# Decay layer of a four-layer graph kernel: counts of two groups share a bank, sums use the array's row halves, and the seams around it are rearranged

## The chip, the core and the metric

The kernel runs on one core of a Trainium2 chip. The metric is the time of one execution on the device in microseconds, as the median of several runs. The core has a matrix engine (PE; its weight loads are listed as PEld), a vector engine (DVE), a scalar engine (ACT), GpSimd (POOL) and a sync engine (SP) that here only issues DMAs. Each of them works through its own queue in order, and they wait for each other by semaphores. PE writes to PSUM, eight banks of 128 partitions x 512 fp32; DVE and ACT read PSUM. SBUF is the memory on the core.

## What is computed

Four layers run one after the other on node features x (4096 x 64) with one adjacency matrix adj (4096 x 4096), and each ends with a layer norm of x plus the layer's output:

```python
x = _layernorm(x + _L0_gnn_ref(x, adj, L0_gnn_weight), axis=-1)   # Chebyshev terms: x, L x, 2 L(..) - .., three products with adj
x = _layernorm(x + _L1_gnn_ref(x, adj, adj, ...), axis=-1)         # attention: products with (adj > 0), (adj < 0) and adj, two GRU cells
x = _layernorm(x + _L2_gnn_ref(x, adj, L2_gnn_weight, L2_gnn_bias), axis=-1)   # decay layer
x = _layernorm(x + _L3_gnn_ref(x, adj, L3_gnn_weight, L3_gnn_bias), axis=-1)   # hyperbolic layer
```

The decay layer, around which the change turns, is

```python
support = input @ weight
mask = (adj != 0)
rank = cumsum(mask, axis=1); deg = rank[:, -1:]
k = minimum(deg, 100.0); pos = rank - (deg - k)
w = mask * where(pos > 0, 0.5 ** (k - pos), 0.0)
out = w @ support + bias                # the kernel sums w @ input first and multiplies by weight after
```

So of each row of adj only the last 100 neighbours count, and each weighs half of the one after it.

## The kernel before

adj is cut into 8 groups of 512 rows, and each group into 8 chunks of 512 columns; a chunk has 4 blocks of 128 columns. Pass 1 (L526 to L575) loads adj chunk by chunk into the pool `rows0` (five buffers of 1 MB), transposes it on PE (L536), copies it out on ACT (L543), reduces it twice on DVE (L569, L571) and writes the transposed chunk to DRAM (L567) for the later layers. The product of the first Chebyshev term runs beside it. The first load is issued by SP at L169, once the constants are set up; the pool takes the SBUF space that the pool `tri` of the constants (L123) has left.

Passes 2 and 3 read the transposed chunks back (`load0`, L587). Pass 3 goes through the groups in the order 7, 0, 1, ..., 6; group g needs chunks g to 0. After a group's matmuls (`halves`, L436) comes `after_third`: the sums are copied out by ACT (`out_of`, L447), weighed and added to what the other terms gave (`times`, L467), normed on DVE (L608, `layernorm`, `centre` with L261, `split` into three bf16 parts L215 to L219), and one group later the result is transposed on PE (`turned_third`, L201). Each of these is put behind the next group's first tile by the small class `Behind`. Group 6, the last, is turned in attention.

Attention (L870 on, in one of two branches chosen by a value of the device) loads the chunks again, makes a mask of the positive entries on DVE (`positives`, L665), writes the mask to DRAM by a POOL DMA (`keep_mask`, L669) and runs three kinds of matmul on it (`wide` L906, 128*128 in the array; `narrow` L914, 128*64; `weighed` L923, 128*64 fp32). When a group's sums are complete, the small work of `group_end` follows in steps, one per chunk; its last step (`decay_parts`) splits the group's layer output into three bf16 parts, hi and mid beside each other in `sup_two`, lo in `sup_lo`.

The decay layer works on four groups at a time (two turns) and from the last column to the first, in 32 blocks of 128 columns a turn, each in two halves of 64 (`h`, odd and even). The count of the neighbours that follow is one matmul with a triangular constant `follow` on the mask, whose result (L1095) is at once the exponent of the weight; the count of group q stands in its own bank `cnt_ps{q}`, in 64 of its partitions (the lower or upper half of the array's columns), and the matmul of the next half block adds to it. The weight is read off the bits: a relu with scale -128 to a 16-bit integer, which is then taken for a bf16 (L1101 on ACT, L1103 on DVE, 64x512 each). So every half block has four count matmuls and four weight operations; ACT does groups 0 and 2 always, and group 3 in every second odd half. Both halves of a block fill one weight tile of 128 partitions, and six steps of two matmuls add the weights times hi, mid and lo to the sums (`gather`, L1064): two groups share a bank `acc_ps{a}`, one in each column half. The gathers of a block are issued among the counts of the next one, by a list `gathers`.

Beside this loop runs a list `seam`, one step a block (L1123): in the first turn the end of attention's last group (22 steps), in the second the ends of the first four groups of the decay layer: `copies` of the sums, `after_decay` for two groups at once (product with the weights L1039, bias, layer norm), `prepare` and `turn_prepared` for the next layer. The ends of the other four groups run in the hyperbolic layer.

The order on each engine is the order of the program as the framework's scheduler settles it; `in_order` pins the marked instructions to the order of the program.

Of the kernel before, what the change touches and what calls it, by code (L numbers as in the profile page):

```python
# [60 lines left out]
def gnn4_kernel(  # L61
# [36 lines left out]


# [60 lines left out]
    def gcols(g):  # L160
        return slice(g * GW, (g + 1) * GW)


    first_p = ctx.enter_context(ExitStack())
    rows_p = first_p.enter_context(tc.tile_pool(name="rows0", bufs=5))

    def load_raw(g, c):
        raw = rows_p.tile([P, GB, CB * P], F32, name="raw", tag="raw")
        nc.sync.dma_start(raw, adj[gcols(g), c * CB * P : (c + 1) * CB * P].rearrange("(b p) j -> p b j", p=P))  # L169
        return raw  # L170

    first_raw = [load_raw(0, NCH - 1)]
# [95 lines left out]
    wd = const.tile([P, 2 * F], F32, name="wd")  # L268
# [10 lines left out]
    def load_decay():  # L279
        nc.vector.memset(wd, 0.0)  # L280
        for q in range(2):
            nc.scalar.dma_start(wd[q * F : (q + 1) * F, q * F : (q + 1) * F], w_dec)
        nc.vector.tensor_scalar_mul(wd, wd, 2.0**DECAY_SHIFT)
        nc.scalar.dma_start(bd, b_dec.partition_broadcast(P))
# [115 lines left out]


# [5 lines left out]
    with first_p, tc.tile_pool(name="acc", bufs=1) as acc_p, tc.tile_pool(name="win", bufs=1) as win_p, tc.tile_pool(  # L407
# [64 lines left out]
        dpart = sm.tile([P, NG, NCH, GB], F32, name="dpart")  # L472
        lows = sm.tile([P, NG * NCH], F32, name="lows")
# [122 lines left out]
        def after_second(g, ps):  # L596
            gs = gblocks(g)
            t_v = out_of(ps, "t_v")
            o = times(new_post(), [(t_v, ident[:, 0:F])])
# [4 lines left out]
        def after_third(g, ps):  # L604
            gs = gblocks(g)
            o = times(new_post(), [(out_of(ps, "t_h"), cheb[:, 3, :]), (acc_t[:, g // 2, :], ident[:, mine(g)])])
# [26 lines left out]
        done = []  # L633
        for n, g in enumerate([NG - 1] + list(range(NG - 1))):
            ps = ps_a.tile([P, GW], F32, name="pass3", tag=("h_ps", "w_ps")[n % 2])
# [5 lines left out]
            while done:  # L641
                turned_third(done.pop())
            later.push(lambda g=g, ps=ps: [after_third(g, ps), done.append(g)])
        later.flush()
        not_turned = done.pop()

    three = ctx.enter_context(tc.tile_pool(name="three", bufs=1))

    nat_c = three.tile([P, NB, F], F32, name="nat_c")
# [6 lines left out]
    sup_two = late.tile([P, NB, 2 * F], BF16, name="sup_two")  # L656
    sup_lo = late.tile([P, NB, F], BF16, name="sup_lo")
    def load1(pool, g, c):
        at = pool.tile([P, CB, GW], F32, name="at1", tag="at")
        nc.sync.dma_start(at, adj_t[g][:, c * CB : (c + 1) * CB, :])  # L660
        return at

    def positives(pool, at):
        pos = pool.tile([P, CB, GW], MASK, name="pos")
        in_order(nc.vector.tensor_scalar(pos, at, 0.0, None, ALU.is_gt, saturate=False))  # L665
        return pos

# [19 lines left out]

# [5 lines left out]
    front = ctx.enter_context(ExitStack())  # L693
    front_p = front.enter_context(tc.tile_pool(name="front", bufs=1))
    with_at = [load1(front_p, NG - 1, c) for c in range(1)]
    with_pos = [positives(front_p, at) for at in with_at]


# [4 lines left out]
    def group_end(g, Q, nb, tl, sums, a_t, wq, by_ln=False):  # L703
# [142 lines left out]
        def decay_parts(ps_p):  # L846

            split(g, nat_b[:, gblocks(g), :], F, sup_two[:, :, 0:F], sup_two[:, :, F : 2 * F], sup_lo)
            nc.vector.tensor_tensor(
                nat_b[:, gblocks(g), :], nat_b[:, gblocks(g), :], bd.unsqueeze(1).to_broadcast([P, GB, F]), ALU.add  # L850
            )
# [18 lines left out]
    def attention(signed, cols_p, sg, tl, ps_a, ps_p):  # L870
# [3 lines left out]
        def masks(g, c):  # L874
            if g == NG - 1 and c < len(with_at):
                at, pos = with_at[c], with_pos[c]
            else:
                at, pos = load1(cols_p, g, c), None
# [17 lines left out]
            up = sg.tile([P, CB, GW], F32, name="up")  # L896
# [34 lines left out]
        else:  # L931
# [5 lines left out]
        lead = 1 if signed else 2  # L937
        ahead = [masks(*order[n]) for n in range(lead)]
        steps = [
            lambda ps_p: to_columns(  # L940
                ps_p, tr_a[0 : F + 1, gcols(not_turned)], nat_a[:, gblocks(not_turned), :], F + 1, nc.scalar.copy
            )
        ]
# [36 lines left out]
    for signed in (True, False):  # L980
        with tc.If(any_negative > 0) if signed else cmp.Else() as block:
            cmp = block
            with tc.tile_pool(name="cols1", bufs=4 if not signed else 2) as cols_p, tc.tile_pool(name="sign1", bufs=2 if signed else 5) as sg, tc.tile_pool(
# [4 lines left out]
                attention(signed, cols_p, sg, tl, ps_a, ps_p)  # L988

    front.close()  # L990
    nc.gpsimd.memset(tr_o, 0.0)
# [40 lines left out]

    decayed = {}

    def after_decay(ps_p, two):

        o = ps_p.tile([P, GB, 2 * F], F32, name="post", tag="post")
        for b in range(GB):
            nc.tensor.matmul(o[:, b, :], lhsT=decayed[two][:, cols(b)], rhs=wd, start=True, stop=True)  # L1039
# [12 lines left out]
    with tc.tile_pool(name="mask2", bufs=3) as mk_p, tc.tile_pool(name="wt2", bufs=3) as wt_p, tc.tile_pool(  # L1052
# [8 lines left out]
        def gather(part, jb, wt, acc, a):  # L1061
            parts = (sup_two[:, jb, 0:F], sup_two[:, jb, F : 2 * F], sup_lo[:, jb, :])
            for q in range(2):
                in_order(nc.tensor.matmul(  # L1064
                    acc[a][q * F : (q + 1) * F, :], lhsT=parts[part], rhs=wt[2 * a + q].bitcast(BF16),
                    start=(jb == NB - 1 and part == 0), stop=(jb == 0 and part == 2), skip_group_check=True,
# [8 lines left out]
        gathers = []  # L1075
        for turn, groups in enumerate(turns_of):
# [433 lines left out]
```

## Time and profile before

| | |
|---|---|
| three runs | 1586.68, 1585.27, 1582.21 us; median 1585.27 |
| the profiled execution | 1581.82 us, its span 1580.0 us, mean granted PE clock 0.968 |
| PE busy | 1418.8 us (90%), 6851 instructions |
| DVE busy | 1166.3 us (74%) |
| ACT busy | 820.1 us (52%) |
| POOL busy | 96.7 us (6%) |
| pass 1, about 12 to 361 us | DMA at 389 GB/s |
| passes 2 and 3, to 597 us | |
| attention, 604 to 887 us | |
| decay layer, 887 to 1108 us | |
| hyperbolic layer, to 1580 us | |

The profile is of one execution. A busy PE is not PE at its peak, since matmuls are pipelined: a matmul of 512 columns lasts some 380 ns in a row of the profile, while the next can start much earlier. The distance of two starts tells more. Rows of groups read: line, engine, operation, tiles out<-in, shape in the array (rows*columns, for PE), operands, count | busy us, mean ns of one | idle time of the engine before them and what ended it.

### The profile page before, as it was taken

Reading aid. Unit: us, or ns where it says so; the run is one execution under the profiler, and the core shown is the slowest. Engines: PE = TensorE matmul, PEld = TensorE weight load, DVE = VectorE, ACT = ScalarE, POOL = GpSimd, SP = SyncE. Lnnn points to the kernel's source line nnn. Section 1 sums busy time; section 2 is a strip of 40 time slices with the busy share of each in tenths; the row PEclk is TensorE's granted clock in tenths of the full one; section 3 lists DMA queues with packets and bytes.
Section 4 is the critical chain, followed back from the end, with each engine's and each line's share of the span. In section 5 each row is a group of like instructions: output and inputs, shape, how many; then the busy total and the mean of one; then the engine's idle time right before and its main releaser. Section 6 shows DMA issues by size and latency. Waiting matters only on the chain.

```text
span 1580.0 us, 19139 instructions
## 1 busy us (share of the span) xinstructions
PE 1418.8 (90%) x6851; PEld 691.3 (44%) x6874; DVE 1166.3 (74%) x2268; ACT 820.1 (52%) x1367; POOL 96.7 (6%) x162
## 2 busy tenths in 40 slices
PE   6899999999998987989999998789789999899995
PEld 4555555554443432333434444445333434344343
DVE  6788988982001534665676688888899999999997
ACT  3444444431000100222222588779888999898895
POOL 3001101000000001111111100000000000000000
PEclk9899999999999998999999999999899999999998
DMA  8999999996776778878978654442425444434430
GB/s 300 409 378 390 413 412 400 379 354 229 249 279 243 265 294 317 300 277 290 333 288 299 201 173 157 137 131 84 182 85 194 153 180 170 163 139 179 162 115 13
DMA packets 102336, 383.81 MB, mean 243 GB/s; under 512 B 15828, under 2 KB 16856, under 8 KB 70232
## 3 DMA queue, kind: packets, MB, share of 16 engines
q1 hardware_dynamic: 84256, 296.78, 52.9%
q0 software_dynamic: 14592, 84.16, 13.0%
q10 hardware_dynamic: 3384, 1.56, 0.5%
q8 instruction: 57, 0.93, 0.2%
q14 instruction: 47, 0.39, 0.1%
HBM read 297.26 MB, written 85.20 MB: 242 GB/s over the span
## 4 chain that ended last, share of the span: by engine, by line
PE 28%; DVE 22%; ACT 6%; DMA 2%; issue 2%; ACTq 0%; DVEq 0%; SPq 0%
PE v_ps L1227 6%; DVE wt L1103 5%; PE sums_ps L1287 4%; PE a_ps L923 3%; PE cnt_ps L1095 3%; DVE rt L1445 2%; DVE at_m L1273 2%; PE acc_ps L1064 2%; DMA at<-adj_t 2%; PE p_ps L906 2%; DVE f L1430 2%; PE post L729 1%; DVE at_d L1433 1%; DVE pos L665 1%; PE post L1271 1%
## 5 line engine op out<-in xcount | busy, mean ns | idle before, releaser
L543 ACT COPY at<-tp 128x512 f32<-128x512 f32 x256 | 133.0, 598 | 151.4 <-issue 106.2
L1101 ACT ACTIVATE wt<-cnt_ps 64x512 uint16<-64x512 f32 x288 | 163.1, 587 | 27.7 <-PE cnt_ps L1095 23.2
L1103 DVE TENSOR_SCALAR wt<-cnt_ps 64x512 uint16<-64x512 f32 x224 | 151.5, 692 | 29.6 <-PE cnt_ps L1095 23.8
L1227 PE MATMUL v_ps<-rv,tr_a 128*128 128x512 f32 (+1 forms) x288 | 142.2, 618 | 33.4 <-DVE rt L1445 32.5
L1095 PE MATMUL cnt_ps<-m,follow 128*64 128x512 fp8e4 x480 | 136.3, 390 | 23.1 <-DVE wt L1103 10.7
L569 DVE TENSOR_REDUCE dpart<-raw 128x4 f32<-128x2048 f32 x64 | 145.4, 2271 | 9.8 <-DMA raw<-in_adj_dram 9.8
L571 DVE TENSOR_REDUCE lows<-raw 128x1 f32<-128x2048 f32 x64 | 145.2, 2269 | 0.0
L536 PE MATMUL tp<-ident,raw 128*128 128x128 f32 x1024 | 133.7, 285 | 8.6 <-DMA raw<-in_adj_dram 8.6
L1287 PE MATMUL sums_ps<-at_d,nat_c 128*64 128x512 f32 x288 | 139.8, 606 | 1.4 <-DVE at_d L1433 1.0
L536 PEld LDWEIGHTS tp<-ident,raw 128*128 128x128 f32 x1024 | 117.2, 146 | 50.2 <-issue 41.2
L923 PE MATMUL a_ps<-at,nat_a 128*64 128x512 f32 x512 | 124.5, 613 | 2.9 <-DVE at L889 2.9
L665 DVE TENSOR_SCALAR pos<-at 128x2048 fp8e4<-128x2048 f32 x72 | 87.0, 1221 | 53.3 <-DMA at<-adj_t 43.4
L1292 PE MATMUL sums_ps<-at_m,nat_c 128*64 128x512 f32 x224 | 108.2, 605 | 0.0
L443 PE MATMUL w_ps<-at,cheb_n 128*128 128x512 f32 x224 | 101.1, 595 | 0.0
L443 PE MATMUL pass<-at,cheb_n 128*128 128x512 f32 x224 | 98.3, 596 | 0.7 <-DVE cheb_n L594 0.7
L1064 PE MATMUL acc_ps<-wt,sup_two 128*64 128x512 bf16 x512 | 96.6, 391 | 0.0
L1227 PEld LDWEIGHTS v_ps<-rv,tr_a 128*128 128x128 f32 x288 | 53.0, 199 | 83.9 <-DVE rt L1445 40.7
L1456 ACT ACTIVATE rt<-rt,one_col 128x1024 f32<-128x1024 f32 x72 | 78.7, 1094 | 17.4 <-DVE rt L1445 17.2
L1445 DVE SCALAR_TENSOR_TENSOR rt<-v_ps,rt 128x1024 f32<-128x1024 f32 x72 | 83.2, 1157 | 3.8 <-ACT rt L1421 3.6
L1430 DVE SCALAR_TENSOR_TENSOR f<-rt,w 128x1024 f32<-128x1024 f32 x72 | 82.8, 1158 | 3.3 <-ACT rt L1456 3.3
L1433 DVE TENSOR_TENSOR at_d<-at_d,f 128x1024 f32<-128x1024 f32 x72 | 83.2, 1156 | 0.1
L1273 DVE TENSOR_TENSOR at_m<-post,at_m 128x512 f32<-128x512 f32 x112 | 74.9, 683 | 9.6 <-PE post L1271 9.1
(346 smaller groups left out, 2262.3 us busy)
## 6 DMA issues: line engine op xcount, KB each, us to landing
at<-adj_t SPq DMA_DIRECT2D x122, 1024.0 KB, 5.2
raw<-in_adj_dram SPq DMA_DIRECT2D x64, 1024.0 KB, 12.1
adj_t<-at POOLq DMA_DIRECT2D x64, 1024.0 KB, 8.2
at_d<-adj_t SPq DMA_DIRECT2D x36, 1024.0 KB, 4.8
at_m<-adj_t SPq DMA_DIRECT2D x28, 1024.0 KB, 6.9
mask_t<-pos POOLq DMA_DIRECT2D x64, 256.0 KB, 6.1
m<-mask_t SPq DMA_DIRECT2D x120, 128.0 KB, 2.8
m<-mask_t SPq DMA_DIRECT2D x60, 256.0 KB, 4.1
```

What stands on the lines that cost most here:

```text
L443: in_order(nc.tensor.matmul(ps, lhsT=cheb_n[:, jb, k : k + 2, :], rhs=rhs, start=first, stop=last))
L536: in_order(nc.tensor.transpose(tp[:, cols(b)], raw[:, b, cols(k)], ident))
L543: nc.scalar.copy(at[:, k, :], tp)
L569: in_order(nc.vector.tensor_reduce(dpart[:, g, c, :], raw, AX.X, ALU.add))
L571: in_order(nc.vector.tensor_reduce(lows[:, n : n + 1], raw.rearrange("p b j -> p (b j)"), AX.X, ALU.min))
L923: in_order(nc.tensor.matmul(ps[q * F : (q + 1) * F, :], lhsT=nat_a[:, c * CB + k, 0:F], rhs=parts[q if signed else 0][:, k, :], start=(c = ...
L1064: in_order(nc.tensor.matmul(acc[a][q * F : (q + 1) * F, :], lhsT=parts[part], rhs=wt[2 * a + q].bitcast(BF16), start=(jb == NB - 1 and par ...
L1095: in_order(nc.tensor.matmul(cnt[q][mine, :], lhsT=follow, rhs=chunks[c][odd][q][:, k, :], start=(h == 2 * NB - 1), stop=True, skip_group_c ...
L1101: in_order(nc.scalar.activation(w, cnt[q][mine, :], AF.Relu, scale=-128.0))
L1103: in_order(nc.vector.tensor_scalar(w, cnt[q][mine, :], -128.0, 0.0, ALU.mult, ALU.max))
L1227: nc.tensor.matmul(vs[n][:, k, cs], lhsT=tr_a[:, cols(jb)], rhs=rights[i][0][:, cs], start=True, stop=True)
L1287: in_order(nc.tensor.matmul(bank[0:F, :], lhsT=nat_c[:, j * CB + k, :], rhs=own[t][:, k, :], start=(i == j and k == 0), stop=(j == seq[-1] ...
```

## The change

In the decay loop the counts of two groups share one bank, one in each half of its partitions, so that one operation of 128x512 makes the weights of both, on ACT for the first pair and on DVE for the second (in the even half of a block with seam work, on ACT for both). A weight tile now holds one half block of two groups, one group in each 64 rows. The sums therefore contract over 64 rows: group r of a pair in row half r of the array, with hi and mid as 128 columns (`gather_two`, 64*128), and lo in a quarter of the array (`gather_lo`, 64*64, four at once in four banks). Each group has a bank of its own for its sums. Since the parts of the input have to lie in both row halves, POOL DMAs copy each half of `sup_two` and `sup_lo` to the other half (`over_two`, `over_lo`).

Beside it: the first load of adj is put ahead of the constants, in a pool on the other side of SBUF; pass 3 takes the groups in the order 7, 0, 6, 1, 5, 2, 4, 3 and does the work after a group by due numbers, counted in tiles (weighing at once, transposing back and norm one tile later, turning five tiles later); attention takes its chunks from the pool of pass 1, and its first four loads and first mask are issued before the rest of pass 3's work; group 6 is no longer turned in attention.

```diff
@@ start
+    rows_p = front.enter_context(tc.tile_pool(name="rows0", bufs=5, side="right"))
+    front_p = front.enter_context(tc.tile_pool(name="front", bufs=1, side="right"))
...
+    first_raw = [load_raw(0, NCH - 1)]
 
     ident = const.tile([P, P], F32, name="ident")
...
-    rows_p = first_p.enter_context(tc.tile_pool(name="rows0", bufs=5))
...
-    first_raw = [load_raw(0, NCH - 1)]
@@ attention's loads
+    def load1(g, c):
+        at = rows_p.tile([P, CB, GW], F32, name="at1", tag="raw")
+        nc.sync.dma_start(at, adj_t[g][:, c * CB : (c + 1) * CB, :])
+        return at
@@ passes 2 and 3
         def after_second(g, ps):
...
-            o = times(new_post(), [(t_v, ident[:, 0:F])])
+            o = new_post()
+            for b in range(GB):
+                nc.tensor.transpose(o[:, b, :], t_v[0:F, cols(b)], ident[0:F, 0:F])
...
-        def after_third(g, ps):
+        def third_weighed(g, ps):
+            o, y_t = weigh(g, [(out_of(ps, "t_h"), cheb[:, 3, :])])
+            nc.vector.tensor_tensor(y_t, o, y_t, ALU.add)
+
+        def after_third(g):
             gs = gblocks(g)
-            o = times(new_post(), [(out_of(ps, "t_h"), cheb[:, 3, :]), (acc_t[:, g // 2, :], ident[:, mine(g)])])
+            o = new_post()
+            for b in range(GB):
+                nc.tensor.transpose(o[:, b, :], acc_t[mine(g), g // 2, cols(b)], ident[mine(g), mine(g)])
...
-        for n, g in enumerate([NG - 1] + list(range(NG - 1))):
+        due, n = [], 0
+        for m, g in enumerate(sum(([NG - 1 - i, i] for i in range(NG // 2)), [])):
...
-            while done:
-                turned_third(done.pop())
-            later.push(lambda g=g, ps=ps: [after_third(g, ps), done.append(g)])
-        later.flush()
-        not_turned = done.pop()
+                while due and due[0][0] <= n:
+                    due.pop(0)[2]()
+                n += 1
+            due += [
+                (n, m, lambda g=g, ps=ps: third_weighed(g, ps)), (n + 1, m, lambda g=g: after_third(g)),
+                (n + 5, m, lambda g=g: turned_third(g)),
+            ]
+            due.sort(key=lambda d: d[:2])
+
+        with_at = [load1(NG - 1, c) for c in range(4)]
+        with_pos = [positives(front_p, with_at[0])]
+        for work in due:
+            work[2]()
@@ decay_parts
             split(g, nat_b[:, gblocks(g), :], F, sup_two[:, :, 0:F], sup_two[:, :, F : 2 * F], sup_lo)
+            for there, here in ((over_two, sup_two), (over_lo, sup_lo)):
+                for q in range(2):
+                    nc.gpsimd.dma_start(
+                        there[(1 - q) * HP : (2 - q) * HP, gblocks(g), :], here[q * HP : (q + 1) * HP, gblocks(g), :]
+                    )
@@ after_decay
-            nc.tensor.matmul(o[:, b, :], lhsT=decayed[two][:, cols(b)], rhs=wd, start=True, stop=True)
+            for q, g in enumerate(two):
+                nc.tensor.matmul(
+                    o[:, b, q * F : (q + 1) * F], lhsT=decayed[g][:, cols(b)], rhs=wd, start=True, stop=True
+                )
@@ decay loop
-        def gather(part, jb, wt, acc, a):
-            parts = (sup_two[:, jb, 0:F], sup_two[:, jb, F : 2 * F], sup_lo[:, jb, :])
-            for q in range(2):
+        def gather_two(jb, half, a, wt, acc):
+            for r in range(2):
+                rows = slice(r * HP, (r + 1) * HP)
                 in_order(nc.tensor.matmul(
-                    acc[a][q * F : (q + 1) * F, :], lhsT=parts[part], rhs=wt[2 * a + q].bitcast(BF16),
...
+                    acc[2 * a + r], lhsT=(sup_two if r == half else over_two)[rows, jb, :],
+                    rhs=wt[half][a][rows, :].bitcast(BF16),
+                    start=(jb == NB - 1 and half == 1), stop=(jb == 0 and half == 0), skip_group_check=True,
+                ))
+
+        def gather_lo(jb, half, wt, acc):
+            for q in range(QG):
+                a, r = divmod(q, 2)
+                rows = slice(r * HP, (r + 1) * HP)
+                to = (a + r) % 2 * F
+                in_order(nc.tensor.matmul(
+                    acc[q][to : to + F, :], lhsT=(sup_lo if r == half else over_lo)[rows, jb, :],
+                    rhs=wt[half][a][rows, :].bitcast(BF16), start=False, stop=False, skip_group_check=True,
                 ))
...
-            cnt = [ps_c.tile([P, GW], F32, name=f"cnt_ps{q}") for q in range(QG)]
-            acc = [ps_a.tile([P, GW], F32, name=f"acc_ps{a}") for a in range(2)]
+            cnt = [ps_c.tile([P, GW], F32, name=f"cnt_ps{a}") for a in range(2)]
+            acc = [ps_a.tile([P, GW], F32, name=f"acc_ps{q}") for q in range(QG)]
...
                 for a in range(2):
-                    for q in (2 * a, 2 * a + 1):
-                        mine = slice(q % 2 * HP, q % 2 * HP + HP)
+                    for r in range(2):
                         in_order(nc.tensor.matmul(
-                            cnt[q][mine, :], lhsT=follow, rhs=chunks[c][odd][q][:, k, :],
+                            cnt[a][r * HP : (r + 1) * HP, :], lhsT=follow, rhs=chunks[c][odd][2 * a + r][:, k, :],
...
-                        w = wt[q][half, :]
-                        if q % 2 == 0 or (q == QG - 1 and h % 4 == 1):
-                            in_order(nc.scalar.activation(w, cnt[q][mine, :], AF.Relu, scale=-128.0))
-                        else:
-                            in_order(nc.vector.tensor_scalar(w, cnt[q][mine, :], -128.0, 0.0, ALU.mult, ALU.max))
-                    for work in [gathers.pop(0) for _ in range(min(len(gathers), 2 - a))]:
-                        work()
+                    if a == 0 or (busy and not odd):
+                        in_order(nc.scalar.activation(wt[odd][a], cnt[a], AF.Relu, scale=-128.0))
+                    else:
+                        in_order(nc.vector.tensor_scalar(wt[odd][a], cnt[a], -128.0, 0.0, ALU.mult, ALU.max))
+                for work in [gathers.pop(0) for _ in range(min(len(gathers), 3))]:
+                    work()
...
+                two = [
+                    lambda half=half, a=a, jb=jb, wt=wt, acc=acc: gather_two(jb, half, a, wt, acc)
+                    for half in (1, 0) for a in range(2)
+                ]
+                lo = [lambda half=half, jb=jb, wt=wt, acc=acc: gather_lo(jb, half, wt, acc) for half in (1, 0)]
+                gathers += lo + two if jb == 0 else two + lo
...
+                        for q, g in enumerate(groups):
+                            decayed[g] = three.tile([P, GW], F32, name=f"sums{q}")
+                            (nc.scalar.copy if q % 2 else nc.vector.tensor_copy)(decayed[g], acc[q])
...
+                busy = bool(seam)
                 if seam:
                     seam.pop(0)(ps_p)
```

## The prediction

> **What bounds the kernel now.** First I cut the span into its stages (busy time in stretches). Columns: PE, PEld, DVE, ACT, POOL busy us, granted clock, DMA share, GB/s.
>
> ```profile
> 12.00:361.00 349.00, 335.27 (x1762) 200.20 (x1763) 302.62 (x247) 154.19 (x303) 34.46 (x65) 0.98 1.01 389
> ...
> 488.00:597.00 109.00, 93.61 (x454) 41.36 (x454) 42.61 (x180) 11.62 (x24) 0.47 (x2) 0.92 0.68 252
> 597.00:604.00 7.00, 0.00 (x0) 0.03 (x1) 6.38 (x25) 0.20 (x1) 0.25 (x1) 0.68 0.95 359
> ...
> 887.00:1108.00 221.00, 194.64 (x1370) 99.57 (x1367) 189.81 (x437) 179.16 (x328) 2.11 (x1) 0.96 0.46 143
> ```
>
> Pass 1 is bound by DMA (share 1.01). Pass 3 (488 to 597) is bound by nothing: PE, DMA and clock all have holes, and seven empty PE microseconds follow before attention. In the decay layer (887 to 1108) three engines are each over 80% busy, so I split it into the first turn, the start of the second (with the ends of the first four groups) and the undisturbed rest:
>
> ```profile
> 889.00:998.00 109.00, 99.87 (x688) 52.18 (x688) 93.72 (x193) 91.61 (x169) 0.11 (x1) 0.98 0.59 182
> 998.00:1043.00 45.00, 30.11 (x205) 14.94 (x206) 40.25 (x158) 26.08 (x52) 0.00 (x0) 0.85 0.40 123
> 1043.00:1101.00 58.00, 56.74 (x426) 28.84 (x423) 50.02 (x80) 54.12 (x97) 0.00 (x0) 1.00 0.35 109
> ```
>
> The groups of the last stretch:
>
> ```profile
> L1101 ACT ACTIVATE wt<-cnt_ps 64x512 uint16<-64x512 f32 x94 | 53.1, 587 | 3.5 <-PE cnt_ps L1095 2.1
> L1103 DVE TENSOR_SCALAR wt<-cnt_ps 64x512 uint16<-64x512 f32 x72 | 48.8, 692 | 8.0 <-PE cnt_ps L1095 6.0
> ```
>
> A block of 128 columns has eight weight operations, 4.5 on ACT and 3.5 on DVE. 4.5 x 0.587 = 2.64 us, and by the starts of each eighth count matmul in the timeline a block takes 2.31 and 3.1 us in turn, 2.70 on average: ACT sets it. A matmul of 512 columns starts every 215 ns, or two column halves together do: twenty halves are 10 x 0.215 = 2.15 us, so PE has 0.55 us over.
>
> **The decay loop.** One 128x512 operation replaces two of 64x512 (L1101, L1103). ACT's full-height 128x512 copies at L447 take 585 ns, so height is free: ACT does 2 x 0.587 = 1.17 us a block, DVE 2 x 0.692 = 1.38. ACT stops being the bound. PE still has ten array slots: four for the counts, four if the eight 64-row sums of hi and mid overlap in pairs, two if four lo sums overlap. But it now changes shape: counts are 128*64, sums 64*128, lo 64*64. In a block that is five changes (counts, sums, counts, sums, lo, counts). The price of a change shows in attention:
>
> ```profile
> 774.84 1.90 PE L906 MATMUL p_ps<-pos,sp_two 128*128 128x512 fp8e4 x8
> 776.66 0.62 PE L914 MATMUL p_ps<-pos,sp_lo 128*64 128x512 fp8e4 x4
> 777.12 1.88 PE L923 MATMUL a_ps<-at,nat_a 128*64 128x512 f32 x8
> ...
> 782.21 1.04 PE L906 MATMUL p_ps<-pos,sp_two 128*128 128x512 fp8e4 x4
> 783.17 0.62 PE L914 MATMUL p_ps<-pos,sp_lo 128*64 128x512 fp8e4 x4
> ```
>
> Eight L906 last 1.82 us to the next shape, four last 0.96: 0.215 each and 0.10 left over for the change. L914 to L923, one shape, has only 0.03 over. So PE needs 2.15 + 5 x 0.10 = 2.65 us, against 2.70: the relief of ACT is spent on changes of shape. The other limit is the circle count, weight, next count in one bank: the matmul pair 0.41, DVE 0.69, and some 0.15 of semaphores, 1.25 us per half block, 2.5 per block, under PE's 2.65. I take 2.70 for the 30 undisturbed blocks, no gain.
>
> No row of before has row halves side by side, nor a change to them. Bounds for a change: 0.03 (one shape to another matmul) to 0.20 (twice the row). I take 0.10. For four lo sums: 0.215 to 0.43 (two pairs); I take 0.215, since pairs of column halves overlap fully here. For a pair of 64-row sums: 0.215 to 0.43 (one after the other); again 0.215.
>
> The Trainium skill (TensorEngine Tiling (Array Packing), Key Properties) says that a change of tiling mode, not merely of tile, drains the engine; the 0.10 us agrees, and it speaks against this edit. The same skill (TensorE: Matmul & The Clock Gate, Measured speedup vs the span model) gives 3.07 times for four row tiles, 77% of four; no run here shows row tiles. By that figure an estimate of the sums of a block is 1.12 + 0.56 us instead of 0.86 + 0.43, and the forecast would be some 1555.
>
> The blocks with other work gain more. In the first 22 blocks the timeline has 78.6 us, 3.4 a block. DVE now does one weight operation there instead of 3.5 (0.69 us instead of 2.42), ACT three (1.76 instead of 2.64); behind ACT's two in an even half the circle is 0.41 + 2 x 0.59 + 0.15 + 0.215 = about 1.5 us, so a block is 1.25 + 1.5 = 2.8, plus PE's gate matmuls (12 of about 0.12 us and two changes) in some: mean 3.05. Gain 22 x 0.35 = 8 us. In the second turn's start the eleven blocks from 998 to 1049 take 51 us. Two of them hold the two layer norms of L1043, some 7.3 us of DVE other than weights, and last 9.9 each; 7.3 + 0.7 and a wait is 8.9. The other nine lose up to 1.7 us of DVE each but keep their transposes and changes: 0.5 each. Gain 2 + 4 = 6. New work is small: four copies of sums in place of two, halved between ACT and DVE (0.59 and 0.69, so as long as before), and twice the L1039 matmuls, 32 more of 0.11 us, half under the seam's DVE. **Decay: -14 us**, from -25 (changes at 0.03) to +12 (changes 0.20, lo 0.43: PE 3.37 us a block).
>
> The copies to the other half (four POOL DMAs a group, 32 in all, at most 192 KB a group) cost POOL 32 x 0.68 us (L669's mean) = 22 us, where POOL is busy 45 of attention's 283; behind them in POOL's queue wait mask writes, which release five mask buffers. The split they wait for stands ahead of the next masks on DVE as well. Zero; if cover fails, 1 us a group, 8.
>
> **The start.** The first load now stands at the head of SP's queue, on the other side of SBUF. Before, it waited for the memory of a constant:
>
> ```profile
> SPq L169 <- DVE follow L135: 11.4, 1, 11.4
> ```
>
> It issued at 12.23 us. What follows is DMA bound, so its end moves with its start, less what the DMAs did in those 12 us anyway: 128 GB/s x 12 us = 1.5 MB, at 389 GB/s 4 us. Gain 11.4 - 4 = 7.4, and x comes a little later beside it: **-7 us** (-10 to -4).
>
> **Pass 3.** It goes from 488.3 to the first attention matmul at 604.1: 115.8 us. Its waits:
>
> ```profile
> PE post L201 <- DVE nat_a L261: 12.2, 5, 4.6
> ...
> PE p_ps L906 <- DVE pos L665: 7.8, 1, 7.8
> ```
>
> PE stands for each group's norm before the transposes of the group; the new due numbers put them five tiles (8.6 us of matmuls) later, past the 4.6. PE's work: 288 instructions x 0.215 = 62; eight weighings of two unpaired 0.43 = 7; 64 transposes x 0.11 = 7; about 40 changes = 4: 80. Loads: 30 tiles of 1.05 MB at 370 GB/s, the best 20 us here (540 to 560), are 85, of which five lie loaded: 70, and the interleaved order (large, small) keeps them going. The end keeps a stall, since the last group's transposes now stand on PE ahead of attention: copy 0.75, weighing 0.9, add 0.7, transposes 0.5, and 4.6 for the norm, 7.4, in place of 7.8. 80 + 7.4 + 8 for waits on loads and clock = 95: **-20 us** (-30, all of the 87.4, to -6, where only the gaps inside go and loads take half of them). Four attention tiles already lie in SBUF then, their SP issues ahead of the late work: **-1 us** (0 to -4), as attention's DMA share, 0.82, makes them up later.
>
> **Sum.** The profiled execution took 1581.8 us (span 1580.0), 3.5 under the median of the three runs and within them. 1581.8 - 14 - 7 - 20 - 1 = 1540.
>
> **Rivals.**
> 1. Changes of shape and lo sums are dear (0.20 and 0.43 us). For: 24 weight loads a block instead of 20, for shapes that cannot be preloaded. Against: the steady 0.10. The decay layer loses 12 and more, +20 with the busy blocks: 1574.
> 2. Pass 3 stays bound by its loads and its last norm; the due numbers hide nothing. For: DMA share 0.97 from 540 to 560. Against: 0.42 from 500 to 520. Then -6 there, 1554.
> 3. Slower: the row halves do not run side by side. Then a block's PE time is 4 + 8 + 4 = 16 slots, 3.44 + 0.5 = 3.94 us, in each of 64 blocks 1.24 over the undisturbed 2.70, less in busy ones: +64 instead of -14, 1618. It decides once the decay layer loses over 28 us, a mean of 0.44 us a block. Against: column halves do overlap here, and the sums go to separate banks.
> 4. Better: pass 3 at 87 and changes hidden behind the waits for weights: 1515.
>
> **Chances.** The forecast (1522 to 1562, rival 2 within it) 0.69, of which rival 2 0.17; rival 1 0.15; rival 3 0.08; rival 4 0.08. The 8-in-10 range reaches from 1512 to 1576: it takes in all low ends (-25, -10, -30, -4 would be 1513) and most of rival 1. A measurement of this kernel tells 0.3% (4.7 us) from no change. Faster: 0.69 + 0.08 + 0.11 of rival 1 = 0.88; same 0.04, of rival 1; slower 0.08.
>
> **What would show it.** First raw load issued before 2 us. Pass 3 with PE waits on L261 under 6 us in total, and attention's first matmul some 27 us earlier than 604. In the decay loop PE with under 5% idle, ACT near 45% and DVE near 55% in undisturbed blocks, 2.65 to 2.75 us apart; sums of the two row halves starting within 50 ns of each other. Starts 215 ns apart inside a pair would be rival 3; 3.3 us blocks with paired starts rival 1. I would be wrong if the scheduler sets the late steps of pass 3 in another order on PE, or if a mask write is late.

## The result and the profile after

The changed kernel takes **1921.39 us** (median of four runs, 1915.52 to 1922.17), the kernel before 1583.84 us (four runs, 1582.21 to 1586.68). The ratio is **1.2121, 95% interval 1.2089 to 1.2153**: slower by 21%, where 1540 us was predicted. The profiled execution took 1915.52 us, its span is 1913.8 us, and its mean granted clock 0.901 (0.968 before).

First the strip of the page that cuts the span into 40 slices of 47.8 us (PE busy, granted clock, DMA, in tenths):

```profile
PE   6899999999976646555555646798898899999995
PEclk9999999999997867677776868899898999999998
DMA  9999999778892433334333334555333244534440
```

The slices 13 to 25, from 574 us to 1196 us, are half empty on PE, at a lower clock, and their DMA stands at 2 to 4 tenths. That is attention, which lasts from 577 to 1220 us. The cut into stages gives the amounts (us, then busy PE, PEld, DVE, ACT, POOL, granted clock, DMA share, GB/s; pass 3, its end, attention, decay layer):

```profile
481.00:564.00 83.00, 77.55 (x360) 27.52 (x360) 43.99 (x182) 10.51 (x22) 0.00 (x0) 1.00 0.91 358
564.00:577.00 13.00, 3.51 (x15) 1.78 (x16) 8.49 (x30) 1.74 (x4) 1.69 (x3) 0.78 0.59 246
577.00:1220.00 643.00, 366.05 (x1242) 130.18 (x1242) 183.23 (x510) 57.37 (x120) 53.54 (x92) 0.75 0.37 128
1222.00:1440.00 218.00, 200.16 (x1638) 68.83 (x1639) 103.86 (x309) 109.86 (x203) 3.31 (x5) 0.96 0.48 146
```

Attention before, in the same columns:

```profile
604.00:887.00 283.00, 260.73 (x1252) 109.44 (x1253) 177.78 (x510) 58.53 (x121) 44.98 (x65) 0.98 0.82 296
```

On PE, DVE and ACT the number of instructions is the same within 1% (POOL has the new copies), but the DMAs move 128 GB/s instead of 296. The sum over the stages of both traces, by their first and last instructions, is: up to pass 3 -7.3 us, pass 3 and its end -20.1, attention +361.6, decay layer -1.9, the rest +1.4; together, before rounding, 333.8, the whole difference of the spans.

What does attention wait for? In the groups of DVE in attention (after the bar: idle time before them, and what ended it) one line has nearly all the waiting for loads, and in the waits of SP's queue one sees what the loads themselves wait for:

```profile
L409 DVE TENSOR_SCALAR pos<-at 128x2048 fp8e4<-128x2048 f32 x71 | 86.8, 1227 | 315.1 <-DMA at<-adj_t 314.5
```

```profile
SPq L404 <- DVE pos L409: 314.6, 55, 18.4
SPq L404 <- PE a_ps L939: 220.9, 54, 12.3
```

So the mask waits for the load, and the next load waits for the last reader of the tile before it (its mask, L409, or its fp32 matmuls, L939). Readers and load take turns. One such turn on PE:

```profile
734.86 1.13 PE L740 MATMUL post<-whh_n,tr_a 128*128 128x256 f32 x4 [0.31 <-ACT gin L837]
738.98 1.86 PE L922 MATMUL p_ps<-pos,sp_two 128*128 128x512 fp8e4 x4 [2.99 <-DVE pos L409]
740.77 1.06 PE L930 MATMUL p_ps<-pos,sp_lo 128*64 128x512 fp8e4 x4
741.63 2.05 PE L939 MATMUL a_ps<-at,nat_a 128*64 128x512 f32 x8
```

and the load behind it, which SP issues 50 ns after the end of the last L939, 743.68:

```profile
743.73 0.32 SPq L404 DMA_DIRECT2D at<-adj_t  x1
```

The load before that one was issued at 732.53 and had landed by 737.70, when its mask began on DVE. From 594.88 us to 1210.66 the trace has 59 loads, 10.6 us apart on average: 4.9 us for a load alone (the page's median from issue to landing, over all 122 loads of these tiles), 1.2 us for the mask, 3 to 5 us of matmuls on this one tile. A pool of five buffers behaves like a pool of one.

The theory from this: **the four tiles loaded ahead of attention never come back while it runs.** They are allocated in front of the two branches of attention and read in both of them, and (so the theory) the framework gives such a tile free only when the whole conditional block ends. The pool `rows0` has five buffers, four are held, and the other 60 tiles of attention go through the fifth. The rivals were: the new POOL DMAs (`over_two`, `over_lo`) stand in front of the mask writes in POOL's queue and hold the loop; or the pool from pass 1, on the other side of SBUF, is itself slow to give buffers back, whoever takes them.

### The profile page after: what moved, and what is told of

It is laid out like the page before. It is cut to its first block, busy times and chain, and to the rows that moved or that the text cites. A ratio compares the mean times of both kernels' runs of the same rounds, so it can differ in the third digit from the quotient of the medians.

```text
span 1913.8 us, 19467 instructions
## 1 busy us (share of the span) xinstructions
PE 1513.0 (79%) x7054; PEld 661.6 (35%) x7054; DVE 1090.1 (57%) x2149; ACT 750.4 (39%) x1243; POOL 109.7 (6%) x194
## 3 DMA queue, kind: packets, MB, share of 16 engines
q0 software_dynamic: 15616, 85.73, 11.2%
## 4 chain that ended last, share of the span: by engine, by line
PE 60%; DVE 18%; DMA 15%; ACT 4%; issue 2%; ACTq 1%; DVEq 0%; SPq 0%
DMA at<-adj_t 12%; PE a_ps L939 8%; PE pass L454 5%; PE tp L547 5%; PE w_ps L454 5%; PE v_ps L1258 4%; PE p_ps L922 4%; PE cnt_ps L1123 4%; PE sums_ps L1318 3%; PE acc_ps L1081 3%; DVE pos L409 3%; PE pass L447 3%; PE h_ps L447 3%; PE p_ps L930 2%; DVE rt L1476 2%
## 5 line engine op out<-in xcount | busy, mean ns | idle before, releaser
L409 DVE TENSOR_SCALAR pos<-at 128x2048 fp8e4<-128x2048 f32 x72 | 88.1, 1227 | 315.1 <-DMA at<-adj_t 314.5
L939 PE MATMUL a_ps<-at,nat_a 128*64 128x512 f32 x512 | 175.2, 821 | 70.1 <-DMA at<-adj_t 55.8
L922 PE MATMUL p_ps<-pos,sp_two 128*128 128x512 fp8e4 x256 | 99.3, 531 | 148.8 <-DVE pos L409 145.4
L1128 ACT ACTIVATE wt<-cnt_ps 128x512 uint16<-128x512 f32 x162 | 93.4, 595 | 87.3 <-PE cnt_ps L1123 86.9
L982 ACT COPY p_t<-p_ps 128x512 f32<-128x512 f32 x7 | 4.1, 585 | 306.1 <-PE p_ps L922 306.1
L1130 DVE TENSOR_SCALAR wt<-cnt_ps 128x512 uint16<-128x512 f32 x94 | 64.9, 690 | 93.0 <-PE cnt_ps L1123 81.1
L939 PEld LDWEIGHTS a_ps<-at,nat_a 128*64 128x64 f32 x512 | 48.4, 191 | 163.9 <-issue 81.1
L930 PE MATMUL p_ps<-pos,sp_lo 128*64 128x512 fp8e4 x256 | 61.5, 572 | 52.3 <-DVE pos L409 52.2
L922 PEld LDWEIGHTS <-sp_two 128*128 128x128 bf16 x256 | 26.9, 116 | 213.1 <-issue 205.9
L1123 PE MATMUL cnt_ps<-m,follow 128*64 128x512 fp8e4 x480 | 78.7, 401 | 17.0 <-DVE wt L1130 9.0
```

The costliest lines, as they stand in the source:

```text
L922: in_order(nc.tensor.matmul(ps[q], lhsT=sp_two[:, jb, :], rhs=two[q][:, k, :], start=(jb == 0), stop=(jb == NB - 1)))
L939: in_order(nc.tensor.matmul(ps[q * F : (q + 1) * F, :], lhsT=nat_a[:, c * CB + k, 0:F], rhs=parts[q if signed else 0][:, k, :], start=(c = ...
L1123: in_order(nc.tensor.matmul(cnt[a][r * HP : (r + 1) * HP, :], lhsT=follow, rhs=chunks[c][odd][2 * a + r][:, k, :], start=(h == 2 * NB - 1) ...
```

## The experiments

The kernel before was run beside these on the same chips; its medians there are 1582.9 to 1585.1 us. Where an interval stands, the kernel ran four to ten times; the others have one time and one profile.

### How many tiles are taken ahead

One tile ahead, everything else as in the change:

```diff
-        with_at = [load1(NG - 1, c) for c in range(4)]
+        with_at = [load1(NG - 1, c) for c in range(1)]
```

> The changed kernel, but one attention tile is loaded ahead of the branch instead of four. Theory 'held': a tile taken from the five-buffer pool ahead of the branch is given back only when the branch ends, so four tiles ahead leave one buffer for the other 60 tiles, and load (4.9 us), mask (1.2) and matmuls follow each other; one tile ahead leaves four buffers, as before. Expected: attention 275 to 290 us instead of 643, total 1545 to 1565 us. Rival 'queue': the four POOL copies of a group stand ahead of the mask writes in POOL's queue, wait for the norm, and the mask buffers run out; then nothing changes here: total over 1880 us.

1557.04 us (1554.61 to 1563.52), ratio to before 0.981, interval 0.9786 to 0.9834: **1.9% faster than before, where four ahead was 21% slower.** One number in one line is worth 364 us. Attention by the same views:

```profile
579.00:867.00 288.00, 262.97 (x1240) 109.51 (x1240) 177.63 (x510) 57.35 (x119) 66.81 (x91) 0.96 0.79 285
```

```profile
L409 DVE TENSOR_SCALAR pos<-at 128x2048 fp8e4<-128x2048 f32 x71 | 85.8, 1224 | 59.9 <-DMA at<-adj_t 59.5
```

The POOL DMAs are still there (91 POOL instructions, 92 with four ahead), and attention runs as before. The rival of POOL's queue falls: in the slow kernel the copies waited

```profile
POOL over_two L862 <- DVE sup_two L219: 88.8, 8, 60.5
```

and with one tile ahead they still wait 64.4 us in six waits, the longest 60.4, without holding attention up.

The sizes between, `range(3)` and `range(2)`:

> The changed kernel with three tiles ahead instead of four. Held: two buffers rotate, each cycle of load 4.9 + mask 1.2 + matmuls some 3.5 us serves two tiles: some 5 us a tile, attention 310 to 350 us, total 1580 to 1630 us. Queue: no change, over 1880 us.

> The changed kernel with two tiles ahead: three buffers rotate. Held by the branch: between three ahead (371 us) and one ahead (288 us), and near the latter, since three tiles' worth of load, mask and matmuls (some 10 us together) come to 3.4 us a tile, under the 4.4 us that a tile takes anyway: attention 285 to 305 us, total 1553 to 1578 us.

1644.95 us and 1586.84 us. DVE's mask with three ahead, and then with two:

```profile
L409 DVE TENSOR_SCALAR pos<-at 128x2048 fp8e4<-128x2048 f32 x71 | 86.7, 1225 | 124.1 <-DMA at<-adj_t 114.2 <-DMA mask_t<-pos 7.7 <-PE p_ps L922 1.7
```

```profile
L409 DVE TENSOR_SCALAR pos<-at 128x2048 fp8e4<-128x2048 f32 x71 | 86.2, 1227 | 81.1 <-DMA at<-adj_t 78.2 <-PE p_ps L930 2.7
```

Each tile that is taken ahead costs a buffer. From the first to the last of attention's L922 matmuls (L906 before):

| taken ahead | buffers left | attention, us | DVE's wait for loads, us |
|---|---|---|---|
| 4 | 1 | 643 | 314.5 |
| 3 | 2 | 371 | 114.2 |
| 2 | 3 | 313 | 78.2 |
| 1 (this run; four more traces below) | 4 | 288 (279 to 284) | 59.5 (52 to 55) |
| before (own pool of four) | 4 | 281 | 43.4 |
| none (below) | 5 | 276 | 14.3 |

For three and for two ahead the direction came as expected, but attention and the total both lie above what was expected (371 against 310 to 350 us, 313 against 285 to 305): two and three buffers cost more than the sums of load, mask and matmuls gave. Three still cost 25 us or more against four.

### The kernel before with one buffer

No branch tile, no `over_two`, no change at all but the size of attention's own pool:

```diff
-tc.tile_pool(name="cols1", bufs=4 if not signed else 2) as cols_p
+tc.tile_pool(name="cols1", bufs=1 if not signed else 2) as cols_p
```

> The kernel before with attention's pool cut from four buffers to one; nothing of the change is in it. Held: the same state as in the changed kernel, attention 600 to 680 us, total 1900 to 1980 us. Queue: the buffers are not what counts, total within 1580 to 1640 us.

1963.38 us, and attention's 658 us look like those of the change: the clock, the DMA share, the rate and the wait are nearly the same.

```profile
606.00:1264.00 658.00, 378.00 (x1244) 133.19 (x1244) 183.15 (x510) 57.75 (x120) 34.55 (x64) 0.74 0.35 128
```

```profile
L665 DVE TENSOR_SCALAR pos<-at 128x2048 fp8e4<-128x2048 f32 x71 | 87.0, 1225 | 331.0 <-DMA at<-adj_t 330.7
```

So one buffer alone gives a loss of that size. What remains is why the four are held.

### Four ahead, but no branch

```diff
-    any_negative = nc.values_load(negatives, min_val=0, max_val=P)
-    for signed in (True, False):
-        with tc.If(any_negative > 0) if signed else cmp.Else() as block:
-            cmp = block
...
+    signed = False
...
+        attention(signed, sg, tl, ps_a, ps_p)
```

> The changed kernel with all four tiles ahead, but without the branch: only the version of attention for matrices without negative entries is in the program (the other version and the test are left out; these inputs take the same path). Theory 'held by the branch': without it the four buffers come back one by one, attention 275 to 295 us, total 1540 to 1565 us. Rival 'held by the pool': the tiles stay taken for another reason than the branch (the list that names them, the pool that is closed after attention); then attention stays at some 640 us and the total over 1880 us.

1547.17 us, one run, at the low end of what the kernel with nothing taken ahead reaches below (1547.2 to 1554.08). The same four tiles from the same pool, and attention takes 276 us:

```profile
575.00:851.00 276.00, 258.21 (x1244) 108.05 (x1244) 175.92 (x512) 58.59 (x121) 70.48 (x91) 0.98 0.82 297
```

```profile
L409 DVE TENSOR_SCALAR pos<-at 128x2048 fp8e4<-128x2048 f32 x69 | 83.0, 1222 | 20.6 <-DMA at<-adj_t 11.2 <-DMA mask_t<-pos 7.0 <-PE p_ps L922 2.0
```

The rival that the pool itself gives buffers back late falls. It is the conditional block that keeps what was allocated before it: without the block, attention takes as long as with nothing taken ahead, and DVE's wait for loads is 11.2 us against 14.3 there. Whether a block with only one branch that reads the tiles would hold them too was not tried. The block also costs PE an idle time in front of attention's first matmul, 3.5 us in the changed kernel and 3.1 with one ahead, that is not there in this run.

### The decay loop by itself

One ahead, and the decay layer of before (counts in four banks, `gather`, no `over_` copies):

```diff
-    sup_two, over_two = [late.tile([P, NB, 2 * F], BF16, name=name) for name in ("sup_two", "over_two")]
+    sup_two = late.tile([P, NB, 2 * F], BF16, name="sup_two")
...
-        def gather_two(jb, half, a, wt, acc):
...
+        def gather(part, jb, wt, acc, a):
```

> As e1, and the decay layer with its operations, its gathers and no POOL copies as in the kernel before. Held: within 6 us of e1 (the decay layers measured 218 and 220 us); total 1545 to 1568 us. Queue: without the copies attention falls to 282 us here while e1 stays over 1880 us. If the new decay loop is worth the 14 us of the prediction, this run is 14 us slower than e1; if its changes of array shape eat the gain, the two are within 5 us.

1552.61 us (1550.77 to 1554.46), ratio 0.9784, interval 0.9759 to 0.9808. With the new loop it was 1557.04: the medians are 4.4 us apart, in favour of the old loop, and the intervals overlap. **The rebuilt decay loop, which gives the change its name, brings no time that these runs show;** this kernel, by its median 2.2% faster than before, is the better of the two. In the traces the layer takes 217.3 us with the new loop and 220.0 with the old one, and most of the 2.7 us is lost behind it: from its end to the first matmul of the hyperbolic layer 5.8 us pass instead of 3.4 (4.9 to 5.8 in all seven traces with the new loop, 3.4 to 3.5 in all six with the old one). Attention before it took 288 us instead of 284, but that code is the same, and with one tile ahead it took 279 to 288 us in five traces.

Where did ACT's relief go? The undisturbed end of the layer in the changed kernel, by stretch and by groups:

```profile
1382.00:1436.00 54.00, 54.00 (x478) 16.27 (x476) 26.75 (x39) 24.51 (x42) 0.00 (x0) 1.00 0.38 118
```

```profile
L1130 DVE TENSOR_SCALAR wt<-cnt_ps 128x512 uint16<-128x512 f32 x38 | 26.3, 691 | 27.0 <-PE cnt_ps L1123 27.0
...
L1128 ACT ACTIVATE wt<-cnt_ps 128x512 uint16<-128x512 f32 x40 | 23.8, 597 | 29.5 <-PE cnt_ps L1123 29.5
```

ACT and DVE are now half idle and wait for the counts alone; PE is busy for 54.00 of 54 us. A block takes 2.74 us (2.70 before). The timeline shows on what PE spends them:

```profile
1405.63 0.40 PE L1093 MATMUL acc_ps<-wt,over_lo 64*64 64x512 bf16 x1
1405.63 0.40 PE L1093 MATMUL acc_ps<-wt,sup_lo 64*64 64x512 bf16 x1
...
1406.18 0.62 PE L1123 MATMUL cnt_ps<-m,follow 128*64 128x512 fp8e4 x4
1406.74 0.39 PE L1081 MATMUL acc_ps<-wt,over_two 64*128 64x512 bf16 x1
1406.74 0.39 PE L1081 MATMUL acc_ps<-wt,sup_two 64*128 64x512 bf16 x1
1406.96 0.38 PE L1081 MATMUL acc_ps<-wt,over_two 64*128 64x512 bf16 x1
...
1407.49 0.62 PE L1123 MATMUL cnt_ps<-m,follow 128*64 128x512 fp8e4 x4
1408.04 0.39 PE L1081 MATMUL acc_ps<-wt,sup_two 64*128 64x512 bf16 x1
...
1408.36 0.40 PE L1093 MATMUL acc_ps<-wt,over_lo 64*64 64x512 bf16 x1
```

Both row halves start at the same time. Within a shape the next pair starts 0.22 us later (1406.74, 1406.96), across a change of shape 0.31 to 0.32 (1408.04, 1408.36). Call the time from one such start to the next a slot. Ten slots of 0.215, five changes of 0.10 (0.094 to 0.105), and 0.011 to 0.025 more for each of the four slots that follow right after a changed one in the same shape come to 2.74.

To measure the price of a change by itself, the lo sums were put between the others, so that a block has seven changes instead of five, with the same matmuls:

```diff
-                gathers += lo + two if jb == 0 else two + lo
+                gathers += lo + two if jb == 0 else two[:2] + lo[:1] + two[2:3] + lo[1:] + two[3:]
```

> As e1, with the gathers of a block in another order (two, two, lo in the first half; two, lo, two in the second): seven changes of array shape a block instead of five, all other work the same. If PE is the bound and a change costs 0.10 us: undisturbed blocks 2.94 to 3.0 us instead of 2.74, the decay layer some 10 to 14 us longer than in e1. Rival: the circle count, weight, next count is the bound and hides the changes; then the blocks stay at 2.74 to 2.8.

1572.16 us (1568.55 to 1573.23), ratio 0.9914, interval 0.9888 to 0.994: 15.1 us over the median of the same kernel with five changes; the decay layer takes 230.3 us instead of 217.3. A block takes 2.97 us, 0.23 more, so 0.115 a change (64 blocks x 0.23 = 14.7). Single sums between two changes now stand 0.32 to 0.34 apart:

```profile
1071.45 0.39 PE L1081 MATMUL acc_ps<-wt,sup_two 64*128 64x512 bf16 x1
...
1071.77 0.40 PE L1093 MATMUL acc_ps<-wt,sup_lo 64*64 64x512 bf16 x1
...
1072.11 0.39 PE L1081 MATMUL acc_ps<-wt,sup_two 64*128 64x512 bf16 x1
...
1072.43 0.62 PE L1123 MATMUL cnt_ps<-m,follow 128*64 128x512 fp8e4 x4
```

And the other limit, the circle of count, weight and next count, is seen when PE has less to do. This kernel leaves out the matmuls of the lo parts:

```diff
-                gathers += lo + two if jb == 0 else two + lo
+                gathers += two
```

> As e1, without the matmuls of the lo parts in the decay layer (its sums lack the third bf16 part). PE work falls by two slots and one change, to some 2.2 us a block. If the circle of 1.25 us per half block is the next bound, undisturbed blocks take 2.45 to 2.6 us; if the circle is shorter than reckoned, 2.2 to 2.3.

1538.33 us. A block takes 2.50 to 2.53 us, and PE now has waits in front of the counts that the full loop had not:

```profile
L1123 PE MATMUL cnt_ps<-m,follow 128*64 128x512 fp8e4 x140 | 22.4, 390 | 3.8 <-ACT wt L1128 3.5 <-DMA m<-mask_t 0.2
```

So with this order of the loop even a PE without any price for changes would not bring the block under 2.5 us: the change had some 0.2 us a block to win there.

### The start and pass 3

Nothing taken ahead, the decay layer of before, the start and pass 3 of the change:

```diff
-        with_at = [load1(NG - 1, c) for c in range(4)]
-        with_pos = [positives(front_p, with_at[0])]
+        with_at = []
+        with_pos = []
```

> As e2 (old decay layer), with no attention tile taken ahead, so that by the theory all five buffers rotate. Attention's first matmul some 5 us later than in e2 (load and mask are no longer ahead), attention itself 0 to 8 us shorter; total 1545 to 1560 us. If buffers beyond four matter, this is the fastest.

1551.86 us (1547.2 to 1554.08), ratio 0.9784, interval 0.9756 to 0.9812: as with one ahead (1552.61). Attention starts 3.4 us later and takes 276 us instead of 284. So a tile loaded ahead moves loading from one side of the seam to the other and gains nothing that these runs show, as long as it also costs a buffer.

The old order of the groups in pass 3, with one ahead and the decay layer of before:

```diff
-        for m, g in enumerate(sum(([NG - 1 - i, i] for i in range(NG // 2)), [])):
+        for m, g in enumerate([NG - 1] + list(range(NG - 1))):
```

> As e2, with pass 3 in the old order of groups (7, 0, 1, ..., 6) but the new due numbers. If the due numbers alone hide the norms, pass 3 stays within 4 us of e2 (1550 to 1558 us in all); if the interleaving of large and small groups is needed to feed the loads and to give five tiles of cover, pass 3 is 6 to 15 us longer.

1557.54 us (1551.64 to 1561.87), ratio 0.9812, interval 0.9785 to 0.984. Pass 3's matmuls take 86.8 us instead of 82.7 us (105.3 before). In the traces the order is worth 4 us of pass 3, and what this run keeps, the due numbers above all, the larger part; the medians (1557.54 against 1552.61) point the same way, but the intervals overlap.

The start alone, in the kernel before: the first load ahead of the constants, its pool on the other side of SBUF.

```diff
+    rows_p = first_p.enter_context(tc.tile_pool(name="rows0", bufs=5, side="right"))
...
+    first_raw = [load_raw(0, NCH - 1)]
+
     ident = const.tile([P, P], F32, name="ident")
```

> The kernel before with one edit: the first load of adj stands ahead of the constants, in a pool on the other side of SBUF. By the prediction 7 us less; by the changed kernel's stages pass 1 ends only 4.6 us earlier. Total 1575 to 1581 us; if the start is worth nothing by itself, within 2 us of the kernel before.

1577.88 us (ten runs, 1574.18 to 1584.16) against 1584.42, ratio 0.9966, interval 0.9946 to 0.9986: 5.4 us, from 2.2 to 8.6. In its profiled execution the first load is issued at 0.8 us instead of 12.2, but pass 1 ends at 362.2 us, as before (362.0); so the gain stands in the medians and is not seen in that one trace. One trace is too coarse for this: with the early load, pass 1 ends between 357 and 359 us in eight traces and between 362 and 363 in three; with the late one, at 362.0 and 365.2.

## Why the prediction was wrong

**The step that failed** is this one: "Four attention tiles already lie in SBUF then, their SP issues ahead of the late work: -1 us (0 to -4), as attention's DMA share, 0.82, makes them up later." It counted what the four loads give and not which buffers they hold. Measured: +361.6 us, since one buffer was left and loads and readers took turns. With the stages as the two traces have them the sum reads 1581.8 - 7 - 20 - 2 + 362 = 1914.8, and the profiled execution took 1915.5. None of the four rivals had this mechanism. The one on the slower side was put on the row halves, which was the new part to the eye; the danger lay in a line that looked free. What could have shown it before: the diff puts attention's 64 tiles into a pool of five that four of them enter outside the block, and in attention of before SP's queue already waited for readers, up to 9.1 us for one tile, so buffers set the pace of the loads even with four:

```profile
SPq L660 <- PE a_ps L923: 156.4, 42, 9.1
```

With that one step mended (one tile ahead) the kernel takes 1557.04 us, 17 us above the forecast of 1540; most of that is the decay term below. Most of the signs that were named came true (the first load, attention's early start, PE without idle time in the decay loop, paired starts), and none of them looked at the step that failed.

**The start**, -7: alone it measured 5.4 (2.2 to 8.6), within the range given. In the changed kernel pass 3 starts 7.3 us earlier, but pass 1 ends only 4.6 us earlier there; the other 2.7 us come in pass 2, whose work after a group was rewritten too and which the prediction gave no time. That the two make 7 is chance.

**Pass 3**, -20: 115.8 us from its start to attention became 95.7, where 95 was worked out. PE's waits for the norm fell from 12.2 us in five waits to 7.5 in three, a little over the 6 us that were named as the sign; the longest is the one foreseen at the end:

```profile
PE post L203 <- DVE nat_a L263: 7.5, 3, 5.4
```

The mechanism was right, and the exact number is in part luck. From the first to the last matmul of the pass it took 82.7 us, where 80 and 8 for waits were worked out, and from there to attention's first matmul 13.0 us, where 7.4 were: the prediction did not have the 3.5 us in front of the conditional block. The rival that loads or the norm would keep pass 3 at its old length falls.

**Decay**, -14: measured -1.9. The undisturbed blocks were right (2.74 against 2.70, price of a change 0.10 to 0.115 against 0.10, both halves side by side), and so the rivals of dear changes and of row halves one after the other fall. The two terms for blocks with other work were mis-sized. The first 22 blocks took 75.4 us, 3.43 on average, where 3.05 was taken (78.6 before): -3 instead of -8. The twelve blocks from the start of the second turn took 59.2 us, 57.4 before: +2 instead of -6 (the 51 us from 998 to 1049, which the prediction gives to eleven blocks, are ten). The two with layer norms lasted 10.2 us, not 8.9 (9.9 before), so taking weights from DVE did not shorten them. The block ahead of the first of them became 1.5 us longer, 5.21 instead of 3.70, with the doubled matmuls of `after_decay` (L1053) in one piece of 1.8 us on PE. The step had taken that work as half hidden; on a PE without idle time it isn't. What sets the 3.43 us of the first 22 is open, but PE's own work has a part in it: they took 69.2 us without the lo sums and 78.5 with seven changes. The 1515 of rival 4 does not follow from its parts either: with pass 3 at 87, the start and the tiles ahead it leaves -30 for the decay layer, below its own low end of -25.

The Trainium skill (TensorEngine Tiling (Array Packing), Key Properties) says that a change of tiling mode drains the engine; the 0.10 to 0.115 us are what a change costs here, for row halves as for column halves. The figure in TensorE: Matmul & The Clock Gate (Measured speedup vs the span model), 3.07 times for four row tiles, is one for tiles of 32 rows, which no run here has, and it did not carry over to 64: the four 64*64 sums start within 10 ns of each other and take one slot, and the estimate of 1555 us by it would have been wrong in its cause.

## What to carry to other kernels

A load that is issued ahead takes a buffer, so ask of each one when that buffer comes back; here a tile that is allocated before a conditional block and used within it was held while the block ran, and four of five held ones made a stage with five buffers serial. Look for one wait pattern: loads that wait for the last reader of the tile before them, while DMA, PE and clock all fall together; here it meant too few free buffers. And when an engine is relieved, work out the limit next to it in the same blocks: here halving ACT's work met a PE bound at the same 2.7 us.

## What the runs showed of the hardware that was not expected

**The clock falls with short gaps.** In attention of the changed kernel 29 groups of four L922 matmuls follow a wait for the mask, of 2.95 to 8.7 us; 28 of them last 1.80 to 1.87 us, where four last 1.04 at full clock. In the five shortest gaps, 2.95 to 3.23 us, the four L922 before the gap had lasted 1.04, so the clock fell in the gap: at 738.98 us PE had been idle since 735.99, and the granted clock is 1.00 up to 738.5 and 0.50 from 738.6 on. So a gap of 3 us could be enough (the one exception followed a gap of 3.44), and PE's busy time in attention rose from 261 to 366 us for nearly the same matmuls: a busy row that grows with the idle one. The Trainium skill (TensorE: Matmul & The Clock Gate, What's actually happening) has the clock halved after an idle window of about 3.4 us; the gaps of 2.95 to 3.23 us here are a little below that.

**A change of shape has a tail.** Besides the 0.10 us at the change itself, the second slot behind it starts 0.24 us after the first instead of 0.215 for counts and lo sums, and 0.226 for the sums of hi and mid.

**Height was free.** A weight operation of 128x512 took 597 ns on ACT and 691 on DVE, one of 64x512 587 and 692.
